# The feed-forward's first product with half of its chunk pairs as seven block products, and sums moved to GpSimd and ScalarE

## The chip, the cores and the metric

The kernel runs on one core of one Trainium2 chip. The metric is the device time of one execution in microseconds, lower is better; the times given are medians of several runs. The engines are TensorE (PE in the profile; its weight loads are listed as PEld), VectorE (DVE), ScalarE (ACT), GpSimd (POOL) and SyncE (SP), which issues most DMAs. Each engine works through its own queue in program order.

## The reference

A block of a transformer on 4096 rows of 256 numbers, in fp32. The input is normalised to `xn`; the result is

```
out = x + attn_ref(xn) + ffn_ref(xn)

attn_ref:  x = layernorm(xn + windowed_attention(xn)) * gamma + beta
           h = gelu(x @ W1 + b1)          # 256 -> 1024
           return x + h @ W2 + b2         # 1024 -> 256

ffn_ref:   scores = softmax(xn @ gate_w.T + gate_b); the two best of 8 experts per row
           y = sum over them of  share * ((silu((xn@gw.T + gb) * (xn@uw.T + ub))) @ dw.T + db)
```

The change lies in the part of `attn_ref` behind the attention (the feed-forward, `gelu(x @ W1 + b1) @ W2`) and in how the experts' results are added to the output.

## The kernel before, in words

All products are fp32; TensorE runs each matmul of the program as two instructions. The kernel has three stages: a first one that normalises the rows, makes the logits and sorts rows by expert; a long middle one that interleaves the experts' units with the attention (the loop over `ALWAYS` blocks, followed by five units that are skipped or run by a flag); and a last one, the feed-forward, which is the loop `for g in range(NG)` at line 1547 with eight groups of 512 rows. The order of the work on every engine is the order in which the program is written (`manual_schedule`, line 140): no planner moves anything.

In the last stage, a group g passes through these steps, and the loop is skewed so that three groups are at work at once:

- `second_loads` (line 1186), two iterations ahead: SP loads `x2`, the attention's output with the residual (two buffers), and `acc`, the rows of the kernel's input, in which the output is summed (four buffers).
- `second_norm` (line 1190): ScalarE applies the layer norm to `x2`, in four activations of 128x256.
- `turned2` (line 1209): TensorE transposes `x2` into two PSUM banks, and ScalarE writes them to `x2T` with gamma and beta.
- `hidden` (line 1222), the first product: eight chunks of 128 hidden units; each is two matmuls with 512 columns into a bank `ph` of its own, followed by a gelu on ScalarE from PSUM to `hT`.
- `second_base` (line 1202): VectorE adds `beta + b2` and `gamma * x2` to `acc`, in three instructions of 128x1024.
- `picked` (line 1266): GpSimd issues eight indirect gathers per group, which fetch each row's two expert results from `done` into tiles `got` of 128x256 (eight buffers, so a group's gathers wait until VectorE has used up the group before).
- `combined` (line 1281): VectorE multiplies each gathered tile by the row's share and adds it to `acc`, in eight instructions of 128x256.
- `sums_of_hidden` (line 1254) and `second` (line 1289): the second product, one group late, as seven products of blocks with a quarter of the size instead of eight (Winograd's form of Strassen's method). Its weight sums `V2` are made once on GpSimd (line 1248, at block `STEPS + 1`); VectorE makes four sums of 128x1024 of the hidden layer per group, and adds the products to `acc`.
- `store`: SP writes `acc` out.

PSUM has a pool of seven banks that the program takes in turn (`bank`, line 129), and one more for the attention. `hidden`, `turned2` and `second` together take 8 + 2 + 7 banks per group.

GpSimd can't begin the gathers of group 0 before the last flagged unit's results are stored; the zeroing of those units' buffers (line 1517) precedes them in its queue.

Of the kernel before, what the change touches and what calls it, by code (L numbers as in the profile page):

```python
# [32 lines left out]
F32 = mybir.dt.float32  # L33
# [3 lines left out]
ALU = mybir.AluOpType  # L37
# [66 lines left out]
def block_kernel(ctx: ExitStack, tc: tile.TileContext, a: dict, out: bass.AP):  # L104
# [1071 lines left out]
    def second_rows(g):  # L1176
        x2 = accp.tile([P, TG, D], F32, tag="x2", name=f"x2_{g}", bufs=2)
        nc.sync.dma_start(out=x2, in_=rows(x1d, g * TG, TG))
        return x2
# [22 lines left out]
    def second_base(g, acc, x2):  # L1202

        scaled = accp.tile([P, TG, D], F32, tag="scaled", name=f"scaled{g}", bufs=1)
        nc.vector.tensor_tensor(acc, acc, bcast(beta_b2, TG, 1), ALU.add)
        nc.vector.tensor_tensor(scaled, x2, bcast(gamma, TG, 1), ALU.mult)
        nc.vector.tensor_tensor(acc, acc, scaled, ALU.add)

    def turned2(g, x2):
        x2T = turns.tile([P, DC, G], F32, tag="x2T", name=f"x2T{g}")  # L1210
        for c in range(DC):
            pt = bank(f"pt2_{g}_{c}")
            for t in range(TG):
                nc.tensor.transpose(  # L1214
                    pt[:, t * P : (t + 1) * P], x2[:, t, c * P : (c + 1) * P], ident
                )
            nc.scalar.activation(
                x2T[:, c, :], pt, AF.Identity, bias=beta_c[:, c : c + 1], scale=gamma_c[:, c : c + 1]
            )
        return x2T  # L1220

    def hidden(g, x2T):
        hT = hf.tile([P, FC1, G], F32, tag="hf", name=f"hf{g}")
        for f in range(FC1):
            ph = bank(f"ph{g}_{f}")
            for c in range(DC):
                nc.tensor.matmul(  # L1227
                    ph,
                    W1[:, c, f * P : (f + 1) * P],
                    x2T[:, c, :],  # L1230
                    start=(c == 0),
                    stop=(c == DC - 1),
                )
            nc.scalar.activation(hT[:, f, :], ph, AF.Gelu, bias=b1[:, f : f + 1])  # L1234
        return hT

# [11 lines left out]
    def sums_of_weights():  # L1248
        b11, b12, b21, b22 = W2[:, F_LO, C1], W2[:, F_LO, C2], W2[:, F_HI, C1], W2[:, F_HI, C2]
        t1, t2, t3, t4 = (V2[:, k] for k in range(4))  # L1250
        for out_, left_, right_ in ((t1, b12, b11), (t2, b22, t1), (t3, b22, b12), (t4, b21, t2)):
            nc.gpsimd.tensor_tensor(out_, left_, right_, ALU.subtract)
# [12 lines left out]

    def picked(g):

        ys = []
        for i in range(g * TG, (g + 1) * TG):
            for k in range(2):  # L1270
                y = got.tile([P, D], F32, tag="got", name=f"got{i}_{k}")
                nc.gpsimd.indirect_dma_start(  # L1272
                    out=y,
                    out_offset=None,
                    in_=done,
                    in_offset=bass.IndirectOffsetOnAxis(ap=slot[:, k, i : i + 1], axis=0),
                )
                ys.append(y)
        return ys

    def combined(g, acc, ys):
        for n, y in enumerate(ys):
            t, k = n // 2, n % 2
            i = g * TG + t
            nc.vector.scalar_tensor_tensor(  # L1285
                acc[:, t, :], y, share[:, k, i : i + 1], acc[:, t, :], ALU.mult, ALU.add
            )

    def second(g, acc, hT, v):

        t1, t2 = slice(0, 2), slice(2, 4)
        u = hf.tile([P, 2, P], F32, tag="u", name=f"u{g}")

        def product(n, left, right):
            pb = bank(f"s{g}_{n}").rearrange("p (t n) -> p t n", n=P)[:, 0:2]
            for t in range(2):
                for f in range(FH):
                    nc.tensor.matmul(  # L1298
                        pb[:, t, :],
                        left[:, f, t * P : (t + 1) * P],  # L1300
                        right[:, f, :],
                        start=(f == 0),
                        stop=(f == FH - 1),
                    )
            return pb

        def add(t, cols, pb):
            nc.vector.tensor_tensor(acc[:, t, cols], pb, acc[:, t, cols], ALU.add)  # L1308

        p1 = product(1, hT[:, F_LO, 0:B], W2[:, F_LO, C1])  # L1310
        nc.scalar.copy(u, p1)  # L1311
        add(t1, C1, u)
        yield
        p2 = product(2, hT[:, F_HI, 0:B], W2[:, F_HI, C1])
        add(t1, C1, p2)
        yield
        p6 = product(6, v[:, 1], V2[:, 1])
        nc.vector.tensor_tensor(u, p6, u, ALU.add)
        add(t1, C2, u)
        yield  # L1320
        p5 = product(5, v[:, 0], V2[:, 0])
        add(t1, C2, p5)
        add(t2, C2, p5)
        yield
        p7 = product(7, v[:, 2], V2[:, 2])
        nc.vector.tensor_tensor(u, p7, u, ALU.add)
        add(t2, C1, u)
        add(t2, C2, u)
        yield
        p3 = product(3, v[:, 3], W2[:, F_HI, C2])  # L1330
        add(t1, C2, p3)
        yield
        p4 = product(4, hT[:, F_HI, B:], V2[:, 3])
        add(t2, C1, p4)
        yield
# [35 lines left out]
    for b in range(ALWAYS):  # L1371
# [63 lines left out]
        if b == STEPS:  # L1435
            att.close()
            wf = pool(ctx, "wf", right)
            accp = pool(ctx, "accp", right, bufs=4)
            V2 = wf.tile([P, 4, FC1 // 2, P], F32, tag="V2", name="V2")
            x2s = {n: second_rows(n) for n in range(2)}  # L1440
            W1, W2 = matrix(wf, "W1", F1, DC), matrix(wf, "W2", D, FC1)
            b1 = column("b1", FC1, wf)
            gamma, beta, b2 = (row(n, D, wf) for n in ("gamma", "beta", "b2"))
            gamma_c, beta_c = column("gamma_c", DC, wf), column("beta_c", DC, wf)
            beta_b2 = wf.tile([P, D], F32, tag="beta_b2", name="beta_b2")
            shift2 = wf.tile([P, NT], F32, tag="shift2", name="shift2")
            turns = pool(ctx, "turns", right, bufs=2)

            late = pool(late_done, "late", right)
            other.update({n: late for n in range(ALWAYS, BLOCKS, 3)})  # L1450
            load_unit(ALWAYS)
            for n in range(ALWAYS, BLOCKS):
                xs[n] = gather(n)
            x2s = {n: (second_inputs(n), x2) for n, x2 in x2s.items()}
        if b == STEPS + 1:
            sums_of_weights()
        if b == ALWAYS - 1:
            load_unit(ALWAYS + 1)
        if b + 1 < ALWAYS:
# [52 lines left out]


    x2Ts = {n: turned2(n, x2s[n][1]) for n in range(2)}

    for b in range(ALWAYS, BLOCKS):
        nc.gpsimd.memset(xs[b], 0.0)
# [18 lines left out]
    late_done.close()  # L1536
    experts_done.close()
    hf = pool(ctx, "hf", right, bufs=2)
    got = pool(ctx, "got", right, bufs=8)
    second_base(0, *x2s[0])  # L1540
    last = None

    def some(steps, n):
        for _ in range(n):
            next(steps, None)

    for g in range(NG):
        if g + 2 < NG:
            x2s[g + 2] = second_loads(g + 2)
        hT = hidden(g, x2Ts.pop(g))  # L1550
        if g + 1 < NG:
            second_base(g + 1, *x2s[g + 1])
        if g > 0:
            acc = x2s.pop(g - 1)[0]
            combined(g - 1, acc, ys)
        if 0 < g < NG - 1:
            x2Ts[g + 1] = turned2(g + 1, x2s[g + 1][1])
        if g + 2 < NG:
            second_norm(g + 2, x2s[g + 2][1])
        ys = picked(g)  # L1560
        outs = second(g - 1, acc, *last) if g > 0 else iter(())
        some(outs, 2)
        sums = sums_of_hidden(g, hT)
        last = hT, next(sums)
        some(outs, 2)
        some(sums, 1)
        some(outs, 3)
        if g > 0:
            store(g - 1, 0, TG, acc)
    acc = x2s.pop(NG - 1)[0]  # L1570
    combined(NG - 1, acc, ys)
    outs = second(NG - 1, acc, *last)
    some(outs, 6)
    store(NG - 1, 0, 2, acc)
    some(outs, 1)
    store(NG - 1, 2, 2, acc)
# [86 lines left out]
```

## Time and profile before

| | |
|---|---|
| median of 3 runs | 1070.18 us (1069.54 to 1071.64) |
| the profiled execution | 1067.22 us, span 1065.5 us |
| the last stage within the span | from 846.8 us to the end |
| ScalarE per gelu from PSUM, 128x512 | 0.687 us |
| VectorE per sum of 128x1024 | 1.22 us |
| VectorE per weighted add of 128x256 (line 1285) | 0.482 us |
| GpSimd per gather of the last stage | 1.008 us in the mean |

The profile is of one execution. A row of a timeline gives the start, the duration, the engine, the line in the kernel, the operation, and output and inputs by the program's names; in brackets follows how long the engine had been idle and what released it. In the chain in order of time the columns are start, duration, engine, tile, line and the number of instructions. A matmul's duration holds its pipeline too, so the distance from start to start tells its cost in a dense run.

### The profile page before, as it was taken

The page shows a single profiled execution, that of the slowest core. Times are in us where ns is not written, and L with a number is a line of the kernel's source. Part 1 is how long each engine was busy: PE and PEld are TensorE (multiplying, and loading weights), DVE is VectorE, ACT ScalarE, POOL GpSimd, SP SyncE. Part 2 cuts the span into 40 slices and gives each one's busy share as a digit, 9 for nine tenths or more (in the row PEclk, how much of TensorE's full clock was granted, in tenths as well). Part 3 has the DMA queues.
Part 4 walks back from the last instruction along what each step waited for, and adds up shares of the span by engine and source line. Part 5 has one row for each costly group of instructions (what it writes and reads, how often), then busy time and mean ns, then how long its engine had stood idle before and what let it go on. Part 6 is the DMA issues. An engine that isn't in the chain of part 4 may idle for free. (4 is left out here: it accounts for less than half of the span.)

```text
span 1065.5 us, 20424 instructions
## 1 busy us (share of the span) xinstructions
PE 1056.0 (99%) x7278; PEld 859.9 (81%) x7278; DVE 755.9 (71%) x1852; ACT 572.0 (54%) x1329; POOL 586.8 (55%) x706
## 2 busy tenths in 40 slices
PE   9999999999999999999999999999999999999998
PEld 6578887887888888888888888888888757777778
DVE  6667876877787687788888988888542455555546
ACT  4527566656656557756665666566454353333320
POOL 5418765675666666776777777777520053222220
PEclk9999999999999999999999999999999999999999
DMA  8226444435345344534543544445585343333111
GB/s 282 81 91 217 140 158 164 165 139 184 120 155 187 111 156 164 193 139 166 173 168 130 189 163 165 139 173 179 179 272 179 134 136 109 100 99 98 61 60 41
DMA packets 61047, 158.67 MB, mean 149 GB/s; under 512 B 6576, under 2 KB 46896, under 8 KB 56208
## 3 DMA queue, kind: packets, MB, share of 16 engines
q1 hardware_dynamic: 53632, 139.33, 37.7%
q0 software_dynamic: 6480, 17.70, 5.2%
q8 instruction: 59, 0.97, 0.4%
q10 hardware_dynamic: 832, 0.30, 0.1%
q14 instruction: 44, 0.36, 0.1%
HBM read 135.43 MB, written 21.89 MB: 148 GB/s over the span
## 5 line engine op out<-in xcount | busy, mean ns | idle before, releaser
L839 PE MATMUL gu<-xsT,wg 128*128 128x256 f32 (+1 forms) x1632 | 362.8, 369 | 0.0
L839 PEld LDWEIGHTS gu<-xsT,wg 128*128 128x128 f32 x1632 | 288.8, 190 | 46.0 <-DVE nm L1057 9.0
L1272 POOL DMA_INDIRECT got<-done,slot x64 | 64.5, 1008 | 175.8 <-DVE acc L1285 106.9
L847 ACT ACTIVATE gs<-gu,wg 128x256 f32<-128x256 f32 (+1 forms) x204 | 92.0, 452 | 112.8 <-PE gu L839 108.4
L1084 POOL TENSOR_TENSOR pr<-pr 128x256 f32<-128x256 f32 x128 | 113.5, 887 | 64.1 <-ACT pr L1072 64.1
L848 DVE SCALAR_TENSOR_TENSOR hT<-gu,wg,gs 128x256 f32<-128x256 f32 (+1 forms) x204 | 91.9, 462 | 73.8 <-ACT gs L847 73.8
L1085 POOL TENSOR_TENSOR pr<-pr,ident 128x256 f32<-128x256 f32 x128 | 132.8, 1038 | 10.0
L1072 ACT ACTIVATE pr<-pr,nm 128x256 f32<-128x256 f32 x256 | 126.8, 497 | 1.0 <-ACT xsT L831 0.6
L1227 PE MATMUL ph<-x2T,W 128*128 128x512 f32 x256 | 111.0, 592 | 0.0
L1234 ACT ACTIVATE hf<-ph,b 128x512 f32<-128x512 f32 x64 | 43.8, 687 | 122.0 <-PE ph L1227 55.3
L880 ACT ACTIVATE hT<-hT 128x512 f32<-128x512 f32 (+2 forms) x179 | 84.9, 485 | 32.6 <-DVE hT L848 22.4
L1057 DVE CUSTOM_DVE_ANT_0 pr<-ps,mask 128x256 f32<-128x256 f32 x256 | 90.7, 420 | 16.1 <-PE ps L1043 16.1
L814 POOL DMA_INDIRECT xs<-xnd,token x71 | 68.8, 969 | 50.7 <-DVE paired_tiles L781 33.1
L1227 PEld LDWEIGHTS ph<-x2T,W 128*128 128x128 f32 x256 | 48.2, 190 | 57.9 <-issue 54.5
L1102 DVE TENSOR_TENSOR pr<-pr,rec 128x1024 f32<-128x1024 f32 x32 | 39.2, 1225 | 42.5 <-POOL pr L1084 42.5
L1115 POOL TENSOR_TENSOR xd<-xd,same 128x256 f32<-128x256 f32 x32 | 19.7, 615 | 84.2 <-DVE same L1113 84.1
L1308 DVE TENSOR_TENSOR acc<-u,acc 128x256 f32<-128x256 f32 x32 | 12.9, 423 | 68.4 <-ACT u L1311 67.9
L929 POOL TENSOR_TENSOR ts<-wd 128x384 f32<-128x384 f32 x54 | 54.0, 1000 | 2.1
L1072 ACT ACT_TABLE_LOAD x31 | 39.8, 1283 | 19.3 <-DVE nm L1057 19.3
L973 ACT COPY y<-sh 128x512 f32<-128x512 f32 x27 | 15.8, 586 | 62.3 <-PE sh L952 62.3
L1072 ACT ACTIVATION_READ_ACCUMULATOR pr<-pr,nm 128x1 f32 x256 | 48.3, 189 | 0.0
L952 PE MATMUL pe<-wd,hT 128*128 128x128 f32 x324 | 44.9, 275 | 0.0
(252 smaller groups left out, 2114.7 us busy)
## 6 DMA issues: line engine op xcount, KB each, us to landing
wg<-in_gate_up SPq DMA_DIRECT2D x37, 1670.5 KB, 7.1
wd<-in_down SPq DMA_DIRECT2D x37, 896.0 KB, 4.7
done<-y SPq DMA_DIRECT2D x30, 256.0 KB, 2.1
x<-in_x SPq DMA_DIRECT2D x8, 512.0 KB, 5.6
xnd<-xn SPq DMA_DIRECT2D x8, 512.0 KB, 4.9
res<-xnd SPq DMA_DIRECT2D x16, 256.0 KB, 2.9
x1d<-res SPq DMA_DIRECT2D x16, 256.0 KB, 2.2
x<-x1d SPq DMA_DIRECT2D x8, 512.0 KB, 4.7
```

The lines of the kernel that those rows point to most:

```text
L814: nc.gpsimd.indirect_dma_start(out=x[:, t, :], out_offset=None, in_=xnd, in_offset=bass.IndirectOffsetOnAxis(ap=token[:, i : i + 1], axis=0),)
L839: nc.tensor.matmul(pb[:, k, :], w[:, lo : lo + P], xT[:, c, :], start=(c == 0), stop=(c == DC - 1),)
L847: nc.scalar.activation(gs, pb[:, 0, :], AF.Identity, bias=w[:, gb : gb + 1])
L848: nc.vector.scalar_tensor_tensor(hT[:, f, :], pb[:, 1, :], w[:, ub : ub + 1], gs, ALU.add, ALU.mult)
L880: nc.scalar.activation(hT[on, lo:hi, :], hT[on, lo:hi, :], AF.Silu)
L929: nc.gpsimd.tensor_tensor(out_, left_, right_, ALU.subtract)
L1057: nc.vector.tensor_tensor_reduce(out=pr[:, hh, j, :], in0=ps[hh][:, j, :], in1=mask[:, kinds[j], :], scale=-1.0, scalar=-LOWEST, op0=ALU.a ...
L1072: nc.scalar.activation(pr[:, hh, j, :], pr[:, hh, j, :], AF.Exp, bias=nm[:, j, hh : hh + 1], scale=-1.0, accum_out=sums[:, j, hh : hh + 1],)
L1084: nc.gpsimd.tensor_tensor(first, first, second, ALU.add)
L1085: nc.gpsimd.tensor_tensor(second, second, bcast(ident, 2, 1), ALU.mult)
L1227: nc.tensor.matmul(ph, W1[:, c, f * P : (f + 1) * P], x2T[:, c, :], start=(c == 0), stop=(c == DC - 1),)
L1272: nc.gpsimd.indirect_dma_start(out=y, out_offset=None, in_=done, in_offset=bass.IndirectOffsetOnAxis(ap=slot[:, k, i : i + 1], axis=0),)
```

## The change

In `hidden`, the eight chunks are taken in four pairs. Pairs 0 and 2 are computed as before. For pairs 1 and 3 the product of the 256x256 weight block with the 256x512 input is made by seven products of 128x128 blocks with 256 columns each, in place of eight; they go to seven halves of four banks. This needs four sums of the weights (`V1`, made once, on GpSimd) and four sums of the input per group (`sums_of_inputs`, on GpSimd, behind `turned2`). The seven products are put together by one copy on ScalarE and five sums on VectorE, which write into `hT`; the gelus of such a pair then run in place on `hT`, behind the next pair's matmuls in the program or, for pair 3, behind the first part of `second`.

`second_base` moves from VectorE (three instructions of 128x1024) to GpSimd (twelve of 128x256). The scaling of the gathered expert results moves to ScalarE (`weighted`: eight activations of 128x256 per group, dealt out between the pairs of `hidden`), and VectorE adds them in two instructions of 128x1024. The gathers get one tile per group with two buffers. In `second`, VectorE's adds of the products p5 and p7 to two places each become one instruction each. The order in the loop changes: `picked` comes directly behind `hidden`, `second_base` of the next group behind it, then `turned2` and `sums_of_inputs` of the next group.

```diff
     def second_base(g, acc, x2):
         scaled = accp.tile([P, TG, D], F32, tag="scaled", name=f"scaled{g}", bufs=1)
-        nc.vector.tensor_tensor(acc, acc, bcast(beta_b2, TG, 1), ALU.add)
-        nc.vector.tensor_tensor(scaled, x2, bcast(gamma, TG, 1), ALU.mult)
-        nc.vector.tensor_tensor(acc, acc, scaled, ALU.add)
+        for t in range(TG):
+            a_, s_ = acc[:, t, :], scaled[:, t, :]
+            nc.gpsimd.tensor_tensor(s_, x2[:, t, :], gamma, ALU.mult)
+            nc.gpsimd.tensor_tensor(a_, a_, beta_b2, ALU.add)
+            nc.gpsimd.tensor_tensor(a_, a_, s_, ALU.add)
...
+    def sums_of_first_weights():
+        m = blocks_of_first()
+        a11, a12, a21, a22 = m[:, 0, 0], m[:, 0, 1], m[:, 1, 0], m[:, 1, 1]
+        s1, s2, s3, s4 = (V1[:, k] for k in range(4))
+        nc.gpsimd.tensor_tensor(s1, a21, a22, ALU.add)
+        for out_, left_, right_ in ((s2, s1, a11), (s3, a11, a21), (s4, a12, s2)):
+            nc.gpsimd.tensor_tensor(out_, left_, right_, ALU.subtract)
+
+    def sums_of_inputs(g, x2T):
+        ts = turns.tile([P, 4, B], F32, tag="x2s", name=f"x2s{g}")
+        b11, b12, b21, b22 = x2T[:, 0, 0:B], x2T[:, 0, B:], x2T[:, 1, 0:B], x2T[:, 1, B:]
+        t1, t2, t3, t4 = (ts[:, k] for k in range(4))
+        for out_, left_, right_ in ((t1, b12, b11), (t2, b22, t1), (t3, b22, b12), (t4, b21, t2)):
+            nc.gpsimd.tensor_tensor(out_, left_, right_, ALU.subtract)
+        return x2T, ts
...
+        def gelu(m):
+            for f in range(2 * m, 2 * m + 2):
+                nc.scalar.activation(hT[:, f, :], hT[:, f, :], AF.Gelu, bias=b1[:, f : f + 1])
+
+        for m in range(FC1 // 2):
+            if m % 2 == 0:
+                pbs = [bank(f"ph{g}_{m}_{k}") for k in range(2)]
+                for k, pb in enumerate(pbs):
+                    for c in range(DC):
+                        nc.tensor.matmul(
+                            pb, w[:, k, c, m, :], x2T[:, c, :], start=(c == 0), stop=(c == DC - 1)
+                        )
+                if m > 0:
+                    gelu(m - 1)
+                for k, pb in enumerate(pbs):
+                    f = 2 * m + k
+                    nc.scalar.activation(hT[:, f, :], pb, AF.Gelu, bias=b1[:, f : f + 1])
+                for _ in range(2 if m == 0 else 1):
+                    next(others, None)
+                continue
+            banks = [halves(bank(f"ph{g}_{m}_{k}")) for k in range(4)]
+            p1, p6, p7, p5, p2, p4, p3 = (banks[k // 2][:, k % 2, :] for k in range(7))
+            for to, left_, right_ in (
+                (p1, w[:, 0, 0, m, :], x2T[:, 0, 0:B]),
+                (p6, V1[:, 1, m, :], ts[:, 1]),
+                (p7, V1[:, 2, m, :], ts[:, 2]),
+                (p5, V1[:, 0, m, :], ts[:, 0]),
+                (p2, w[:, 0, 1, m, :], x2T[:, 1, 0:B]),
+                (p4, w[:, 1, 1, m, :], ts[:, 3]),
+                (p3, V1[:, 3, m, :], x2T[:, 1, B:]),
+            ):
+                nc.tensor.matmul(to, left_, right_, start=True, stop=True)
+
+            q = hf.tile([P, 3, B], F32, tag="q", name=f"q{g}_{m}", bufs=3)
+            both = hT[:, 2 * m : 2 * m + 2, :]
+            nc.scalar.copy(q[:, 0], p1)
+            nc.vector.tensor_tensor(q[:, 1], p6, q[:, 0], ALU.add)
+            nc.vector.tensor_tensor(q[:, 2], p7, q[:, 1], ALU.add)
+            nc.vector.tensor_tensor(both[:, :, B:], q[:, 1:3], bcast(p5, 2, 1), ALU.add)
+            nc.vector.tensor_tensor(both[:, :, 0:B], banks[2], q[:, 0::2], ALU.add)
+            nc.vector.tensor_tensor(both[:, 0, B:], p3, both[:, 0, B:], ALU.add)
+            next(others, None)
+        return hT, lambda: gelu(FC1 // 2 - 1)
...
+    def weighted(g, ys):
+        for t in range(TG):
+            for k in range(2):
+                i = g * TG + t
+                nc.scalar.activation(
+                    ys[:, k, t, :], ys[:, k, t, :], AF.Copy, scale=share[:, k, i : i + 1]
+                )
+            yield
+
+    def combined(acc, ys):
+        for k in range(2):
+            nc.vector.tensor_tensor(acc, acc, ys[:, k], ALU.add)
...
     for g in range(NG):
         if g + 2 < NG:
             x2s[g + 2] = second_loads(g + 2)
-        hT = hidden(g, x2Ts.pop(g))
+        hT, ended = hidden(g, *x2Ts.pop(g), weighted(g - 1, ys) if g > 0 else iter(()))
+        ys_last = ys if g > 0 else None
+        ys = picked(g)
         if g + 1 < NG:
             second_base(g + 1, *x2s[g + 1])
+        if 0 < g < NG - 1:
+            x2Ts[g + 1] = sums_of_inputs(g + 1, turned2(g + 1, x2s[g + 1][1]))
+        acc = x2s.pop(g - 1)[0] if g > 0 else None
         if g > 0:
-            acc = x2s.pop(g - 1)[0]
-            combined(g - 1, acc, ys)
-        if 0 < g < NG - 1:
-            x2Ts[g + 1] = turned2(g + 1, x2s[g + 1][1])
+            combined(acc, ys_last)
+        outs = second(g - 1, acc, *last) if g > 0 else iter(())
+        some(outs, 1)
+        ended()
         if g + 2 < NG:
             second_norm(g + 2, x2s[g + 2][1])
-        ys = picked(g)
-        outs = second(g - 1, acc, *last) if g > 0 else iter(())
-        some(outs, 2)
+        some(outs, 1)
         sums = sums_of_hidden(g, hT)
```

Behind the loop, the last group's eight scalings stand in front of its `second`, and its `combined` behind the first two products. `sums_of_first_weights` is called at block `STEPS + 1`, behind `sums_of_weights`; the first two groups' `sums_of_inputs` stand behind their `turned2` at line 1514, in front of the zeroing at line 1517.

More of the change, by code (lines that the diff above doesn't have):

```diff
@@ L1220, in turned2, with blocks_of_first @@
         return x2T
-    def hidden(g, x2T):
-        hT = hf.tile([P, FC1, G], F32, tag="hf", name=f"hf{g}")
[L1224 to L1235, printed above, removed]
+    def blocks_of_first():
+        return W1.rearrange("p c (m e q) -> p e c m q", e=2, q=P)
@@ new lines, in hidden @@
+    def hidden(g, x2T, ts, others):
+        hT = hf.tile([P, FC1, G], F32, tag="hf", name=f"hf{g}")
+        w = blocks_of_first()
+        def gelu(m):
[39 more added lines that the diff above has]
+        return hT, lambda: gelu(FC1 // 2 - 1)
@@ L1266, in picked @@
     def picked(g):
-        ys = []
-        for i in range(g * TG, (g + 1) * TG):
+        ys = got.tile([P, 2, TG, D], F32, tag="got", name=f"got{g}")
+        for t in range(TG):
+            i = g * TG + t
             for k in range(2):
-                y = got.tile([P, D], F32, tag="got", name=f"got{i}_{k}")
                 nc.gpsimd.indirect_dma_start(
-                    out=y,
+                    out=ys[:, k, t, :],
                     out_offset=None,
@@ L1277, in picked @@
                 )
-                ys.append(y)
         return ys
[L1281 to L1287, printed above, removed]
+    def weighted(g, ys):
+        for t in range(TG):
+            for k in range(2):
+                i = g * TG + t
+                nc.scalar.activation(
[5 more added lines that the diff above has]
+            nc.vector.tensor_tensor(acc, acc, ys[:, k], ALU.add)
     def second(g, acc, hT, v):
@@ L1321, in second @@
         p5 = product(5, v[:, 0], V2[:, 0])
-        add(t1, C2, p5)
-        add(t2, C2, p5)
+        right = acc.rearrange("p (k t) d -> p k t d", k=2)[:, :, :, C2]
+        nc.vector.tensor_tensor(right, right, bcast(p5, 2, 1), ALU.add)
         yield
@@ L1326, in second @@
         nc.vector.tensor_tensor(u, p7, u, ALU.add)
-        add(t2, C1, u)
-        add(t2, C2, u)
+        low = acc[:, t2, :].rearrange("p t (h n) -> p t h n", h=2)
+        nc.vector.tensor_tensor(low, low, bcast(u, 2, 2), ALU.add)
         yield
@@ L1439, in block_kernel @@
             V2 = wf.tile([P, 4, FC1 // 2, P], F32, tag="V2", name="V2")
+            V1 = wf.tile([P, 4, FC1 // 2, P], F32, tag="V1", name="V1")
             x2s = {n: second_rows(n) for n in range(2)}
@@ L1456, in block_kernel @@
             sums_of_weights()
+            sums_of_first_weights()
         if b == ALWAYS - 1:
@@ L1514, in block_kernel @@
     x2Ts = {n: turned2(n, x2s[n][1]) for n in range(2)}
+    x2Ts = {n: sums_of_inputs(n, x2T) for n, x2T in x2Ts.items()}
     for b in range(ALWAYS, BLOCKS):
@@ L1538, in block_kernel @@
     hf = pool(ctx, "hf", right, bufs=2)
-    got = pool(ctx, "got", right, bufs=8)
+    got = pool(ctx, "got", right, bufs=2)
     second_base(0, *x2s[0])
@@ L1570, in block_kernel @@
     acc = x2s.pop(NG - 1)[0]
-    combined(NG - 1, acc, ys)
+    list(weighted(NG - 1, ys))
     outs = second(NG - 1, acc, *last)
-    some(outs, 6)
+    some(outs, 2)
+    combined(acc, ys)
+    some(outs, 4)
     store(NG - 1, 0, 2, acc)
```

## The prediction

> **What bounds the kernel now.** I read the page's busy times, then the chain in order of time, then the engines' timelines in the last stage, and last the groups by shape.
>
> ```profile
> PE 1056.0 (99%) x7278; PEld 859.9 (81%) x7278; DVE 755.9 (71%) x1852; ACT 572.0 (54%) x1329; POOL 586.8 (55%) x706
> ```
>
> TensorE is busy throughout. The chain says where that decides:
>
> ```profile
> 846.76 27.47 PE ph L1227 x64
> 874.22 0.87 PE pt L1214 x8
> 875.10 12.51 PE s L1298 x112
> 887.60 13.73 PE ph L1227 x32
> ...
> 1023.18 13.73 PE ph L1227 x32
> 1036.92 25.03 PE s L1298 x224
> 1061.94 0.02 issue
> 1061.97 0.42 DVE acc L1308
> ```
>
> From 846.8 to 1062 us one TensorE piece follows another: the first product (ph), turns (pt), the second product (s), 13.73 + 0.87 + 12.51 = 27.11 us for a group of 512 rows, without a gap. Everything else there is covered today, so whatever shortens TensorE shortens the kernel, unless another engine's cover is used up. So I look at GpSimd and VectorE:
>
> ```profile
> 850.15 1.50 POOL L1272 DMA_INDIRECT got<-done,slot  x1 [56.10 <-DVE scaled L1206]
> 851.95 1.94 POOL L1272 DMA_INDIRECT got<-done,slot  x1 [0.30 <-issue]
> 854.20 0.95 POOL L1272 DMA_INDIRECT got<-done,slot  x1 [0.30 <-issue]
> ...
> 860.46 0.95 POOL L1272 DMA_INDIRECT got<-done,slot  x1 [0.30 <-issue]
> 870.20 1.07 POOL L1272 DMA_INDIRECT got<-done,slot  x1 [8.80 <-DVE acc L1285]
> ```
>
> GpSimd does nothing here but issue eight gathers a group, one each 1.25 us (0.95 and a 0.30 gap), 10 us of 27. It can't begin before the experts' last results are stored, at 850.2.
>
> ```profile
> 256.51 0.72 POOL L1084 TENSOR_TENSOR pr<-pr 128x256 f32<-128x256 f32 x1
> 257.26 1.23 DVE L1102 TENSOR_TENSOR pr<-pr,rec 128x1024 f32<-128x1024 f32 x1 [0.22 <-POOL pr L1084]
> 257.31 1.77 POOL L1085 TENSOR_TENSOR pr<-pr,ident 128x256 f32<-128x256 f32 x1
> ```
>
> A GpSimd sum of 128x256 takes 0.72 us alone, and 1.77 us where it starts just behind a 1024-wide VectorE sum of two SBUF tensors: it stands still for 1.0 us, most of that instruction.
>
> **The change, part by part.** *TensorE.* Two of a group's four chunk pairs change from 8 instructions of 512 columns to 14 of 256. The 512s follow each other at 13.73/32 = 0.429 us. For 256s I take the expert units' dense run at line 839: 48 from 810.72 to 821.17, 0.218 us. So 3.43 becomes 3.05: 0.38 saved, 16 times, 6.1 us in all; a group is then 26.35 us. With nothing in the way: 1067.2 - 6.1 = 1061.1 in the profiled execution's terms (span 1065.5 and 1.7 around it), and 1064.1 against the median of 1070.2, which lies 3.0 above.
>
> *ScalarE.* For eight gelus from PSUM (0.687 each) come four from PSUM, four from SBUF (about 0.63, by the silu of that shape, line 880), two copies (0.364, line 1311) and eight scalings of 128x256 (0.52, by line 1194: four in 2.07). With line 1217's two (1.44), line 1194's four and one u copy, 14 us of 26. No table load lies between gelu and copy in the trace. The order matters more: block copy p1 stands behind two gelus and four scalings, so in a group that starts at 0 it comes at 6.4 (its product ended at 3.9), VectorE's five sums end at 9.4, the pair's gelus at 10.8, the next plain pair's at 12.0. TensorE needs that last bank at 13.8 for the second product. So 1.6 us of slack; in group 1, where norms and gelus crowd, it is gone, and I take 0.2 us there.
>
> *VectorE.* Off it go second_base (three times 1.22) and eight 0.48 sums; onto it come ten block sums (0.42 for 256, 0.68 for 512 from PSUM, by lines 1308 and 1124), about 5.3 us, and two 1.22 sums. About 17 of 26 us: covered.
>
> *GpSimd* is the part that I cost at more than nothing. A group adds twelve base sums and four input sums of 128x256. Rows for such a sum: 0.615 (line 1115, an operand repeated), 0.73 with 0.75 start to start (lines 1084 and 1085 alone); 128 and 384 wide start 0.415 and 1.07 apart, between them 0.74. I take 0.74, ends 0.68 and 0.75. So a group needs 10.0 + 16 x 0.74 = 21.8 us alone. To it come the standstills: VectorE's sums of two SBUF tensors are six of 1024 (four for the hidden layer, two of combined), 1.0 us each, two of 256 at 0.3 and one of 512 at 0.5: 7.1 us if all meet a GpSimd sum. Block sums have one operand in PSUM, and GpSimd's 384-wide sums stay at 1.00 beside VectorE's PSUM work (lines 929 and 1057), so they cost nothing. Bounds for the group: 21.8 and 28.9.
>
> Would gathers be stopped too? The Trainium skill (SBUF — State Buffer, "Who interferes with whom") infers that tensor_tensor doesn't hold back descriptor generation. The rows above differ: the two gathers under lines 1205 to 1207 took 1.50 and 1.94 instead of 0.95, some 0.5 us per VectorE sum; yet one at 879.33 beside line 1258 took 0.94. By the rule gathers stay 1.25 apart; by the first rows group 1's set costs 1.5 us more. I follow the rule, since most gathers will lie beside block sums.
>
> *When it bites: the input sums of group 2.* They stand last in GpSimd's queue. From 850.2: gathers of group 0, 10.0, to 860.2; base of group 1, 8.9, with the four hidden sums of group 0 falling into it, 4.0, to 873.1; gathers of group 1 to 883.1; base of group 2, 8.9 + 2.8 (two hidden sums and the smaller ones), to 894.8; the second input sum, 1.5, at 896.3. TensorE wants it for its second block product: 846.8 + 12.97 (group 0) + 26.35 + 0.2 + 3.87 = 890.2. **A stall of 6.1 us.** Even without standstills GpSimd would be there only at 889.5. Behind that product stand all of TensorE's later work and, through its banks, ScalarE and VectorE.
>
> *After that.* Having once waited for GpSimd, TensorE runs a fixed distance behind it: the next gathers lie under the block sums, and combined, hidden sums and adds all fall into the next base sums. By the sum, 28.9; a walk through one group's order gives 28.7 with 0.74 and 27.5 to 27.9 with quicker sums. I take 28.2, so 28.2 - 26.35 = 1.85 us of waiting in each of groups 3 to 7, 9.3 us.
>
> *Hidden.* The V1 sums (four 512-wide, 1.3 each, line 1252) and the first two input sums (5.9) run in GpSimd's idle time from 795 to 850; base of group 0 follows and ends near 825; the zeroing passed by them is needed at 822.7 by the first store and is done by 815. Without that cover they would push the first gathers. SP's x2 loads now wait for GpSimd's base sums, which in the walk are done some 12 us before the norm on ScalarE. The merged adds save VectorE about a microsecond, off the path. The tail keeps its order: last product, add, store.
>
> The sum: -6.1 + 0.2 + 6.1 + 9.3 = +9.5, or **1079.7 us** against the median, and 1076.7 for a profiled execution.
>
> A second rule speaks against the change: by the skill (TensorE: Matmul & The Clock Gate, Part 1) an idle window of about 3.4 us halves the clock until TensorE was busy as long. The granted clock is 1.00 in every stretch of this stage, which has no such pause; my 6.1 us one would be the first. At half clock for 3.4 us it costs an estimated 1.7. While GpSimd sets the pace TensorE has that to spare, so 9.5 stands; where TensorE sets it, add 1.7.
>
> **The rivals.** *GpSimd keeps up.* If VectorE mostly finds GpSimd between sums, or sums take 0.6, group 2's inputs come in time, only ScalarE's 0.2 remains, and the time is 1064. For it: 21.8 us of need against 26.35. Against: the 1.77 row, and that 889.5 against 890.2 leaves no room. *One stall and no more:* with half the standstills (groups of 25.4 us) the stall is 2.7 to 5, -6.1 + 0.2 + 4 + up to 1.7, around 1070. This decides at a GpSimd group under 26.35, that is standstills under 4.5 us. *ScalarE sets the pace:* if scalings or SBUF gelus cost about 0.3 more each, the 1.6 us of slack is passed in each group; at 2 us more, 8 x 2 - 6 = +10 without GpSimd, and up to 1090 with it. The copies between gelus in the trace speak against it. *That the block products don't save:* weights load in 0.19 us, under 0.218; at 0.245 each nothing would be left. Dense 256s at 0.218 exclude it.
>
> **How the numbers follow.** GpSimd sets the pace 0.53 (its own range 1075 to 1086: sums of 0.68, a 5 us stall and 27.5, or 7.5 us and 28.9); GpSimd keeps up 0.18; one stall 0.20, of which 0.05 faster, 0.08 within, 0.07 slower; ScalarE 0.09. Within 0.2% (2.1 us, about what a measurement of this kernel can tell from none) 0.08; faster 0.18 + 0.05 = 0.23; slower 0.69. The range from 1065 to 1087 leaves out the lower part of the second case and the upper ends of the first and last, under 2 in 10.
>
> **What would show it.** In the chain of the changed kernel: GpSimd's input sums ahead of the ph pieces from group 2 on; TensorE waiting for ts near 890, for 4 to 8 us, then 1 to 2.5 us a group; GpSimd busy nearly all of 850 to 1010; base sums with a mean near 1.0 and single ones near 1.77; block products 0.218 apart. A gapless TensorE chain with 26.35 us groups would prove me wrong, as would TensorE waiting for gelus or u copies instead.

## The result

| | median | runs | ratio to before |
|---|---|---|---|
| before | 1070.12 us (1069.54 to 1071.64) | 4 | |
| after | 1078.57 us (1078.12 to 1078.83) | 4 | 1.0077, 95% interval 1.0063 to 1.0091 |

The change makes the kernel slower by 8.4 us; 1079.7 was predicted. The profiled execution of after took 1078.55 us, at its median (span 1076.8); that of before lay 3 us under its own median, so the two spans differ by 11.3 us. 1.5 of these lie ahead of the last stage, where both kernels run the same TensorE work: in the chain the first product starts at 848.30 now, at 846.76 before.

**The page of after**, busy times and the row of the granted TensorE clock:

```profile
PE 1056.8 (98%) x7374; PEld 880.3 (82%) x7374; DVE 773.1 (72%) x1844; ACT 601.0 (56%) x1409; POOL 719.3 (67%) x838
...
PEclk9999999999999999999999999999999998999999
```

GpSimd went from 55% to 67%, and TensorE from 99% to 98% with less to do. For the first time there is a slice at 8 in the clock's row.

**The chain of after in order of time** was a gapless row of TensorE pieces before. From 874 to 1038.6 us it is now GpSimd's (start, duration, engine, tile, line; other links are left out):

```profile
POOL 13%; PE 6%; issue 2%; DVE 0%; POOLq 0%
...
927.79 0.99 POOL got L1332
...
955.89 0.99 POOL got L1332
...
984.01 0.99 POOL got L1332
...
1012.16 0.99 POOL got L1332
...
1038.64 3.11 PE ph L1284 x12
1041.75 3.43 PE ph L1262 x8
1045.18 3.02 PE ph L1284 x14
1048.21 25.02 PE s L1362 x224
```

The first gathers of successive groups start 28.10, 28.12 and 28.15 us apart. TensorE takes over only for the last first product and the tail. The last two ph rows give the saving: seven block products in 3.02 us, a plain pair in 3.43.

**GpSimd's timeline of after** shows where 28.1 us come from:

```profile
862.84 0.73 POOL L1209 TENSOR_TENSOR acc<-acc,scaled 128x256 f32<-128x256 f32 x1
863.53 0.73 POOL L1207 TENSOR_TENSOR scaled<-x,gamma 128x256 f32<-128x256 f32 x1
864.22 1.76 POOL L1208 TENSOR_TENSOR acc<-acc,beta_b 128x256 f32<-128x256 f32 x1
...
874.12 0.99 POOL L1332 DMA_INDIRECT got<-done,slot  x1
875.42 0.95 POOL L1332 DMA_INDIRECT got<-done,slot  x1 [0.30 <-issue]
```

Some sums take 0.73 us, and some, beside a 1024-wide VectorE sum of two SBUF tensors, 1.59 to 1.78: the means of the three base sums are 1.21, 1.26 and 1.12 us. VectorE is slowed in return: its four sums of the hidden layer, 1.22 us each before, take 1.26 to 1.68 in the mean (1.22 again in the run below that leaves the base sums on VectorE). The gathers keep 1.25 us from start to start.

**TensorE's timeline of after** has three things in it: short pauses with no wait shown, one wait followed by slow products, and one wait a group from group 5 on:

```profile
882.74 0.27 PE L1362 MATMUL s<-V,hv 128*128 128x128 f32 x1 [0.17 <-issue]
883.47 0.27 PE L1362 MATMUL s<-V,hv 128*128 128x128 f32 x1 [0.46 <-issue]
884.85 0.39 PE L1362 MATMUL s<-V,hv 128*128 128x128 f32 x2 [1.12 <-issue]
885.59 2.06 PE L1362 MATMUL s<-V,hv 128*128 128x128 f32 x17 [0.35 <-issue]
...
898.57 2.93 PE L1284 MATMUL ph<-x2s,V 128*128 128x256 f32 x6 [3.48 <-POOL x2s L1243]
901.29 1.06 PE L1284 MATMUL ph<-x2T,W 128*128 128x256 f32 x2
...
908.16 1.46 PE L1284 MATMUL ph<-x2s,V 128*128 128x256 f32 x6
...
982.55 1.82 PE L1284 MATMUL ph<-x2s,V 128*128 128x256 f32 x6 [1.31 <-POOL x2s L1243]
...
1010.70 1.82 PE L1284 MATMUL ph<-x2s,V 128*128 128x256 f32 x6 [1.33 <-POOL x2s L1243]
...
1038.64 1.82 PE L1284 MATMUL ph<-x2s,V 128*128 128x256 f32 x6 [1.13 <-POOL x2s L1243]
```

The wait of group 2 is 3.48 us, for the input sums, as foretold in kind. Behind it the same six instructions take 2.93 us instead of 1.46. The waits of groups 5 to 7 cost more than their brackets: the sums then come some 0.7 us apart, and the six instructions need 1.82.

**Stretches of after around that wait** (per stretch: length, busy time of PE, PEld, DVE, ACT and POOL with instructions, granted clock, DMA share, GB/s):

```profile
894.00:898.00 4.00, 1.09 (x4) 0.38 (x2) 0.94 (x3) 2.28 (x5) 3.84 (x6) 0.99 0.48 140
898.00:904.00 6.00, 5.43 (x13) 4.32 (x14) 2.23 (x4) 1.18 (x3) 4.94 (x7) 0.50 0.66 213
904.00:908.00 4.00, 4.00 (x11) 1.78 (x10) 0.42 (x1) 2.10 (x4) 3.09 (x4) 0.91 0.36 102
908.00:914.00 6.00, 6.00 (x44) 5.62 (x43) 4.13 (x7) 3.51 (x8) 5.59 (x7) 1.00 0.21 66
```

The clock is at half from 897.90 to 904.72, for 6.8 us. From 898.57 to the next first block product at 907.72 TensorE needed 9.15 us for work that takes 12 x 0.216 + 3.43 = 6.02 at full clock: 3.1 us lost.

### The profile page after: what moved, and what is told of

Same layout as the page of the kernel before. It is cut to its first block, busy times and chain, and to the rows that moved or that the text cites. A ratio compares the mean times of both kernels' runs of the same rounds, so it can differ in the third digit from the quotient of the medians.

```text
span 1076.8 us, 20832 instructions
## 1 busy us (share of the span) xinstructions
PE 1056.8 (98%) x7374; PEld 880.3 (82%) x7374; DVE 773.1 (72%) x1844; ACT 601.0 (56%) x1409; POOL 719.3 (67%) x838
## 5 line engine op out<-in xcount | busy, mean ns | idle before, releaser
L1332 POOL DMA_INDIRECT got<-done,slot x64 | 60.9, 952 | 48.1 <-issue 47.1
L1262 PE MATMUL ph<-x2T,W 128*128 128x512 f32 x128 | 58.0, 596 | 0.0
L1269 ACT ACTIVATE hf<-ph,b 128x512 f32<-128x512 f32 x32 | 21.3, 680 | 61.4 <-PE ph L1262 60.1
L1289 DVE TENSOR_TENSOR q<-ph,q 128x256 f32<-128x256 f32 x16 | 6.8, 424 | 61.9 <-ACT q L1288 36.2
L1362 PE MATMUL s<-V,hv 128*128 128x128 f32 x384 | 44.8, 275 | 2.1 <-issue 2.1
L1362 PEld LDWEIGHTS s<-V,hv 128*128 128x128 f32 x384 | 43.8, 192 | 2.4 <-issue 2.0
```

The lines of the kernel that those rows point to most:

```text
L1262: nc.tensor.matmul(pb, w[:, k, c, m, :], x2T[:, c, :], start=(c == 0), stop=(c == DC - 1))
L1332: nc.gpsimd.indirect_dma_start(out=ys[:, k, t, :], out_offset=None, in_=done, in_offset=bass.IndirectOffsetOnAxis(ap=slot[:, k, i : i + 1] ...
L1362: nc.tensor.matmul(pb[:, t, :], left[:, f, t * P : (t + 1) * P], right[:, f, :], start=(f == 0), stop=(f == FH - 1),)
```

## The experiments

The theory: GpSimd's need for a group is over TensorE's, and TensorE waits for the input sums, which stand last in GpSimd's queue. Rivals: something else slows TensorE, and the waits for GpSimd would otherwise be filled by it; or another part of the change costs the time.

**The base sums back on VectorE.** All else of the change stays.

```diff
-        for t in range(TG):
-            ...   (three sums of 128x256 on nc.gpsimd)
+        nc.vector.tensor_tensor(acc, acc, bcast(beta_b2, TG, 1), ALU.add)
+        nc.vector.tensor_tensor(scaled, x2, bcast(gamma, TG, 1), ALU.mult)
+        nc.vector.tensor_tensor(acc, acc, scaled, ALU.add)
```

> The changed kernel with the base sums back on VectorE, in three instructions of 128x1024 at the same place. GpSimd then has 10.0 us of gathers and 3.0 us of input sums a group, and VectorE about 21 of 26 us. GpSimd theory: no wait for input sums, 1064 to 1068. ScalarE theory: 1077 to 1080. If VectorE becomes the bound by the 3.6 us that come back to it, TensorE waits for banks that block sums hold, some 0.5 to 1 us a group: 1070 to 1075.

1062.67 us against 1068.58, ratio 0.9944 (0.9928 to 0.9961). The waits of TensorE in the last stage are this one line (total us, times, longest):

```profile
PE pt L1214 <- ACT hf L1267: 0.7, 1, 0.7
```

Groups are 26.3 us apart. VectorE, busy for 21.7 of 27 us, is not in the way. Run once more:

> The version with the base sums on VectorE once more beside the others, to tell small differences: 1061.5 to 1064 beside a kernel before of 1067 to 1070.

1062.22 us, 0.9956 (0.9943 to 0.9970). So the base sums on GpSimd turn a gain of 5 to 6 us into a loss of 8.4.

**The base sums alone moved to GpSimd**, in the kernel before:

> The kernel before with one part of the change alone: the base sums on GpSimd in twelve instructions; products, gathers, adds and their order as before. GpSimd theory: 10.0 us of gathers, 8.9 of sums and up to 7 of standstills are under the 27.1 us of a group, and nothing that TensorE needs soon stands behind them; 1068 to 1072. If moving the base sums is costly as such: 1076 to 1080.

1067.59 us against 1067.35, ratio 1.0003 (0.9994 to 1.0012). There nothing on TensorE waits for GpSimd, and the same move costs nothing. It is the input sums behind the base sums that give GpSimd's queue a reader on the path.

**One more base sum a block** (four a group):

```diff
-            nc.gpsimd.tensor_tensor(s_, x2[:, t, :], gamma, ALU.mult)
+            for _ in range(2):
+                nc.gpsimd.tensor_tensor(s_, x2[:, t, :], gamma, ALU.mult)
```

> The changed kernel with the product of x2 and gamma made twice on GpSimd: 16 base sums a group for 12, the same output. GpSimd theory with 0.74 us a sum: 2 x 4 x 0.74 = 5.9 us later at group 2 and 5 x 3.0 us after it, 14.7, together 20.7: 1097 to 1101, with a GpSimd group of 31.1 us. ScalarE theory, or any in which GpSimd is hidden: 1078 to 1080.

1097.93 us, ratio 1.0271 (1.0253 to 1.0288). TensorE's timeline in this run:

```profile
901.56 2.93 PE L1285 MATMUL ph<-x2s,V 128*128 128x256 f32 x6 [10.36 <-POOL x2s L1244]
...
932.57 1.95 PE L1285 MATMUL ph<-x2s,V 128*128 128x256 f32 x6 [1.87 <-POOL x2s L1244]
```

Every group from 2 on now waits, and gathers start about 30.9 us apart. Four more sums a group lengthen it by 2.8 us: what GpSimd gets, the kernel pays.

**More VectorE work of two kinds**, behind p5's add, to tell the standstill apart from VectorE's own load: two 1024-wide sums of an SBUF tile with itself (1.60 us each as measured, 3.2 a group), or six 256-wide sums with p5 in PSUM (0.417 each, 2.5 a group). The first edit, then the second (the tile `spare` is made and zeroed ahead of the loop):

```diff
+        for _ in range(2):
+            nc.vector.tensor_tensor(spare, spare, spare, ALU.add)
```

```diff
+        for n in range(6):
+            w_ = spare[:, n % TG, :].rearrange("p (t n) -> p t n", t=2)
+            nc.vector.tensor_tensor(w_, p5, w_, ALU.add)
```

> The changed kernel with two more VectorE sums of 128x1024 a group behind the add of p5, both operands in SBUF (a tile of zeros added to itself), the same output. VectorE has the time: some 21 of 28 us a group. [...]each stops a GpSimd sum for 1.0 us, so group 2's inputs come 2 us later and each of the five groups behind it takes 2 us more: 10 to 12 us, 1088 to 1091. If the long GpSimd sums of the profile have another cause (a slow form, or the two sums' dependence), VectorE's idle time takes the new work: 1078 to 1080.

> The control to the two sums of SBUF tensors: in their place six VectorE sums of 128x256 of about the same time together (2.1 us a group), each with one operand in PSUM (the product p5) and one in SBUF. [...]they don't stop GpSimd, 1078 to 1081. If added VectorE time in itself is what delays GpSimd or TensorE: 1088 to 1091, as with the two sums.

The first: 1088.16 us, 1.0191 (1.0174 to 1.0209). The second: 1077.03 us, 1.0094 (1.0077 to 1.0111), which overlaps the change's own interval. The waits of the first, then of the second:

```profile
PE ph L1284 <- POOL x2s L1243: 19.0, 7, 8.7
```

```profile
PE ph L1284 <- POOL x2s L1243: 10.7, 4, 7.0
```

Gathers start 29.8 us apart in the first, 28.0 in the second. VectorE's added time is not far apart, 3.2 and 2.5 us; it costs GpSimd 0.9 us per 1024-wide sum where the operands are in SBUF, and nothing where one is in PSUM. So the standstill goes with VectorE's sums of SBUF tensors, as the prediction took from one row, and not with VectorE's load (though the two kinds differ in width as well).

**The input sums ahead of the base sums**, so that TensorE finds them early although GpSimd has the same work:

```diff
         ys = picked(g)
-        if g + 1 < NG:
-            second_base(g + 1, *x2s[g + 1])
         if 0 < g < NG - 1:
             x2Ts[g + 1] = sums_of_inputs(g + 1, turned2(g + 1, x2s[g + 1][1]))
+        if g + 1 < NG:
+            second_base(g + 1, *x2s[g + 1])
```

> The changed kernel with two lines of the loop exchanged: the next group's input sums stand in front of its base sums in GpSimd's queue, so that TensorE's block products wait for 8 gathers and 4 sums where they waited for 12 sums more. Nothing is left out. GpSimd theory: group 2's inputs are ready near 887 where TensorE asks near 893, and GpSimd's lag of about 1.8 us a group never uses up the 12 us gained; no wait for the input sums, no half clock, a time of 1064 to 1068. If it is GpSimd's load as such that sets the pace, whatever stands last (a group of 28.1 us against 26.3), the waits come back by the last groups: 1070 to 1074. ScalarE theory (its scalings and the gelus in place delay the banks): 1077 to 1080, as before the exchange.

1069.14 us against 1068.58, ratio 1.0003 (0.9994 to 1.0011): over what was expected. The waits for the input sums are gone and the clock is 1.00 throughout, but TensorE's waits are now

```profile
PE s L1362 <- issue: 4.0, 8, 0.9
PE pt L1216 <- ACT hf L1269: 0.5, 1, 0.5
```

and the groups from group 1 on are 3.4, 1.1, 1.3, 0.7, 0.0 and 0.7 us over 26.3. 1.1 of the first lie in its turns, as with the base sums on VectorE (27.39 us there); for the other 6.1 us the trace shows no wait. The pauses are all in the second product, like those at 882.7 in after.

**Block products that read the turned input itself.** Left out: the input sums as operands, so the hidden layer is another one; GpSimd still makes the sums, and nobody waits for them.

```diff
-                (p6, V1[:, 1, m, :], ts[:, 1]),
+                (p6, V1[:, 1, m, :], x2T[:, 0, B:]),
```

(p7, p5 and p4 likewise.)

> The changed kernel with the four block products that read input sums reading blocks of the input itself instead; every sum is still made on GpSimd, with the same instructions on every engine, but TensorE doesn't need them. Left out: the use of the input sums, so the hidden layer is another one. GpSimd theory: TensorE's groups are 26.3 us throughout, 1064 to 1068, and GpSimd's queue still takes about 28 us a group. ScalarE theory: 1077 to 1080.

1068.56 us, ratio 0.9999 (0.9990 to 1.0008): missed in the same way. No waits for GpSimd; 3.0 us of pauses without a releaser in six places, and behind the first two of them the clock at half for 3.4 us (884.46 to 887.87). So the theory covers the waits, but in these two runs a second cost shows once the waits are gone.

**Where does the second cost come from?** The record gives the chip of each run but after: both of these were on chip 10, those below on 12 and 7. In both runs these pauses lie around the end of a group's eight gathers (in the run with the input sums first, from 1.0 us before the eighth ends to 1.6 behind), while TensorE is in the second product. The next idea was that gathers under the second product starve TensorE. So, with the base sums on VectorE, the gathers were moved there on purpose:

```diff
-        ys = picked(g)
         if g + 1 < NG:
             second_base(g + 1, *x2s[g + 1])
         if 0 < g < NG - 1:
             x2Ts[g + 1] = sums_of_inputs(g + 1, turned2(g + 1, x2s[g + 1][1]))
+        ys = picked(g)
```

> The version with the base sums on VectorE, with one more move: GpSimd issues a group's gathers behind the next group's input sums in place of ahead of them, so that they run some 17 to 27 us behind a group's start, under the dense second product, and no longer under the first. The same instructions, the same output. Theory that TensorE's instructions come late while gathers run under the second product (the gaps of 0.4 to 1 us without a wait that the traces of the two versions without input waits show there, some 0.7 us a group): gaps come back in groups 1 to 6, 1066 to 1069. If those gaps belong to the base sums on GpSimd beside TensorE's reads, none come: 1062 to 1064. If instead the scalings wait for their gathers, ScalarE stands in front of the block copies and the time is 1064 to 1072, but with waits that the trace puts down to gathers.

1061.95 us against 1067.48, ratio 0.9954 (0.9939 to 0.9970), and no pause: the idea fell as it stood, as far as a run on another chip can tell. But the gathers were not the same ones. GpSimd's timeline there:

```profile
879.63 1.77 POOL L1330 DMA_INDIRECT got<-done,slot  x1
881.71 0.95 POOL L1330 DMA_INDIRECT got<-done,slot  x1 [0.30 <-issue]
```

12 of 56 gathers from group 1 on take over 1.3 us, as those two rows show one that does and one that doesn't; in after none of 64 does.

The same with plain loads in place of the gathers (left out: the choice of rows, so other rows of the experts' results are added):

> As the late gathers, but each gather is a plain load of the same size (128 rows of 1 KB) on ScalarE's queue. Left out: the choice of rows, so other experts' results are added. If the bytes moved under the second product hold up TensorE's instructions, the gaps stay, 1065 to 1070; if it is the gathers' own descriptors[...], they go, 1062 to 1064.

1061.38 us, 0.9947 (0.9931 to 0.9962), no pauses either, as with gathers; this pair tells nothing apart.

The order that does have the pauses, input sums first, was then run with plain loads instead of gathers. Left out again: the choice of rows.

```diff
-                nc.gpsimd.indirect_dma_start(out=ys[:, k, t, :], ...)
+                nc.scalar.dma_start(out=ys[:, k, t, :], in_=done[i * P : (i + 1) * P, :])
```

> As the run with the input sums first, but the gathers of the other experts' rows are plain loads of 128 rows each on ScalarE's queue at the same place. Left out: the choice of rows, so other rows of the experts' results are added. If the gathers issued by GpSimd at full pace under the second product are the ingredient of TensorE's gaps there: the gaps (4.0 us in 8) go, and the time is 1062 to 1065 us. If the base sums on GpSimd beside the other engines' reads are enough: the gaps stay, 1067 to 1070 us.

1061.08 us against 1067.54, ratio 0.9939 (0.9922 to 0.9955). First TensorE's second product of group 0, then two stretches:

```profile
877.53 5.52 PE L1357 MATMUL s<-V,hv 128*128 128x128 f32 x48
...
901.00:928.00 27.00, 27.00 (x173) 22.42 (x172) 19.01 (x28) 12.93 (x26) 16.91 (x16) 1.00 0.33 102
928.00:955.00 27.00, 27.00 (x173) 22.42 (x172) 19.02 (x26) 13.17 (x27) 17.39 (x17) 1.00 0.35 107
```

and the same two of the run with gathers:

```profile
901.00:928.00 27.00, 26.08 (x164) 21.52 (x163) 18.09 (x25) 12.17 (x25) 24.32 (x25) 1.00 0.35 108
928.00:955.00 27.00, 26.25 (x163) 21.39 (x162) 17.81 (x25) 11.97 (x25) 24.01 (x26) 1.00 0.35 105
```

The 48 matmuls with hv run in one piece, TensorE is never idle, and no pause is left, though the base sums are on GpSimd, the order is the same and the DMAs move about as many bytes a second. This points at the gathers, but it doesn't show them to be an ingredient. The run with the pauses was on another chip (10) than this one (7), and without gathers GpSimd's sums also begin some 3 us earlier within a group. A run on a third chip (6) speaks against it: the one with six PSUM sums is the changed kernel, gathers and all, up to the first sum that was added. TensorE there, and then one of GpSimd's gathers:

```profile
877.09 5.52 PE L1362 MATMUL s<-V,hv 128*128 128x128 f32 x48
...
897.01 2.93 PE L1284 MATMUL ph<-x2s,V 128*128 128x256 f32 x6 [6.95 <-POOL x2s L1243]
```

```profile
877.54 1.85 POOL L1332 DMA_INDIRECT got<-done,slot  x1 [0.30 <-issue]
```

The 48 matmuls that take 8.2 us in after, from 879.40 on, take 5.5 here without a pause, and two of the gathers beside them are held (1.85 and 1.88 us; in after none is). The run with two more SBUF sums, on the same chip, has no such pauses either. Nor are the pauses common to chip 10: the runs there with the base sums on VectorE and with four more base sums have none.

The trace shows one thing more: around a pause TensorE's word that a product is done comes late. In after, VectorE adds the product p2, the second half of the first row here, 5.3 us after its end, though VectorE was free from 882.28 on. In the run with the input sums first, the product p1 that began at 931.4 ended at 933.3, and ScalarE, idle since 932.6, copies it at 937.27:

```profile
875.72 3.84 PE L1362 MATMUL s<-W,hf 128*128 128x128 f32 x32
884.90 0.42 DVE L1372 TENSOR_TENSOR acc<-s,acc 128x256 f32<-128x256 f32 x1 [2.62 <-remote]
```

```profile
937.27 0.37 ACT L1375 COPY u<-s 128x256 f32<-128x256 f32 x1 [4.67 <-remote]
```

Semaphores are the counters by which the engines tell each other what is done. The traces record TensorE's updates only just ahead of these two starts, at 884.87 and 937.25. The traces of after and of the four runs on chip 10 also lack 30 to 90 of some 600 semaphore updates in the last stage; those of all other runs lack none. So the pauses go with late and missing semaphore updates. Whether they belong to the kernel, to one chip or to the recording of the trace stays open: the order with the input sums first was run with its gathers on one chip only.

**One more pair as block products** (pairs 1, 2 and 3), with the base sums on VectorE; each block pair's gelus follow the next pair's sums:

```diff
-            if m % 2 == 0:
+            if m == 0:
```

> The version with the base sums on VectorE, with pairs 1, 2 and 3 of each group as block products in place of 1 and 3; the same output. By the block products' measured spacing 0.41 us less in each group, 3.3 us in all: 1059.5 against the 1062.7 of two pairs. Against it VectorE's 2.7 us more a group, about 24 of 25.9 us: where block sums then come late for the banks, 1062 to 1068.

1060.47 us against 1067.48, ratio 0.9931 (0.9918 to 0.9945). It is the lowest ratio of the runs that compute the whole layer, and faster than both kernels; against the version with two pairs (0.9944, 0.9956) the intervals overlap, so the third pair's own gain isn't shown. TensorE has 1.7 us of waits for VectorE's block sums, in group 1:

```profile
PE ph L1279 <- DVE hf L1286: 1.3, 1, 1.3
PE ph L1279 <- DVE q L1284: 0.4, 1, 0.4
```

Behind these two waits the clock is at half for 3.4 us (from 872.00 on; the rows are in the last section), an estimated 1.7 us more. So in group 1 the third pair gives back most of the 3.3 us that were forecast for it.

## Why the prediction was right

The sum was -6.1 + 0.2 + 6.1 + 9.3 = +9.5. The time came out within 1.1 us, and by the mechanism that was named. The terms:

*The block products, -6.1.* 3.43 - 3.02 = 0.41 a pair, 6.6 us. Right; and with neither waits nor pauses the change does gain this much: the run with the input sums first and plain loads has a ratio of 0.9939, 6.5 us.

*ScalarE, +0.2.* One wait for a bank in group 1, 0.58 us. Right in place, somewhat small. There is no other: the rival that ScalarE sets the pace is out.

*GpSimd's queue up to group 2.* The walk, with what was measured: gathers of group 0 end at 860.2 (861.3), base of group 1 at 873.1 (874.1), gathers at 883.1 (883.9), base at 894.8 (897.0), the second input sum at 896.3 (898.5). The later start accounts for the first microsecond; the base of group 2 took 13.1 us and not 11.7, since two more of its sums met a standstill.

*The stall, +6.1.* Here the sum was mis-sized: 3.48 us. The step that failed is "846.8 + 12.97 (group 0) + 26.35 + 0.2 + 3.87 = 890.2". TensorE asked at 895.1: 1.5 us from the later start, 0.4 from the bank, and 2.8 because its second product of group 0 took 15.3 us and not 12.5, through the pauses, which no step of the prediction had. GpSimd came 2.2 us later than forecast, so 6.1 + 2.2 - 4.9 = 3.4. The pauses cost nothing here, since TensorE would have waited for GpSimd instead. In the run with six PSUM sums, which has no pauses, TensorE asks at 890.05 and gets the sums at 897.01, where the forecast had 890.2 and 896.3: a wait of 6.95 us.

*The clock.* The rule of the Trainium skill (TensorE: Matmul & The Clock Gate, Part 1) was put at 1.7 us. This case agrees that a pause halves the clock and differs in the size: 3.1 us, since the clock stayed at half for 6.8 us and not 3.4. That it would be to spare held: GpSimd's period stayed at 28 us, and TensorE, 3 us behind, met no wait of note in groups 3 and 4.

*1.85 us in each of groups 3 to 7, +9.3.* The step per group is confirmed nearly to the digit: GpSimd needs 28.1 us (28.2 said), and with TensorE's 26.3 the groups that waited were longer by 1.83, 1.84 and 1.65. It came in groups 5 to 7 only, with half a microsecond in group 4. So the waits came to some 9 us and not 15.4, and pauses and half clock took the rest of the time. The end didn't change, because it was counted along GpSimd's queue: 896.3 + 5 x 28.2 = 1037.3 said for the last input sums, 1038.6 found, with a start 1.5 later.

*Gathers.* Taking them as not held back, by the rule (SBUF — State Buffer, "Who interferes with whom"), fits after: 0.952 us in the mean, none of the 64 over 1.3, even beside combined's two sums at 879.3 to 881.8. As a rule it does not hold here: beside the same two sums, gathers took 1.85 and 1.88 us in the run with six PSUM sums, and with the gathers moved behind the input sums, 12 of 56 took up to 1.87 us.

*The rivals.* "GpSimd keeps up" (1064) is what one gets with the base sums on VectorE. What the prediction lacked is that removing the waits alone would not get there: with TensorE no longer waiting, it would have said 1064 to 1068, and 1069.1 was measured, level with before on that chip.

## What to carry to other kernels

When work moves to an engine with idle time, add up that engine's period including standstills and compare it with the bound's; then look at what stands last in its queue, for that decides whether the surplus is paid. Moving the sums cost nothing in the kernel before and 13 to 14 us where TensorE read a tile made behind them. A forecast made along the queue that becomes the bound survives errors about the other engines; the split into their waits does not, and taking one wait away may uncover the next cost. A control for such a cost has to run where the cost was seen: on another chip it may be missing for another reason.

## What the runs showed of the hardware

- **Pauses far below 3.4 us halve the clock, and it is a matter of where they lie.** Within the last stage of each trace the clock stays at half for 3.41 us or a multiple of it, and its changes are multiples of 3.41 us apart (in the run with four more base sums it falls at 934.12, 964.84 and 995.56, nine times 3.41 apart each time). Stretches of that length, in the run with four more base sums (a pause of 1.87 us) and in the one with three pairs (pauses of 0.43 and 1.26 us):

```profile
930.71:934.12 3.41, 1.55 (x6) 1.09 (x7) 0.41 (x1) 2.69 (x8) 3.19 (x6) 1.00 0.85 238
934.12:937.53 3.41, 3.41 (x9) 2.46 (x8) 2.23 (x5) 0.36 (x1) 2.79 (x3) 0.50 0.68 211
```

```profile
868.59:872.00 3.41, 1.72 (x7) 0.90 (x6) 2.65 (x6) 0.00 (x0) 2.80 (x3) 1.00 0.35 106
872.00:875.41 3.41, 3.41 (x10) 2.69 (x9) 3.17 (x9) 2.87 (x6) 1.51 (x2) 0.50 0.43 115
```

  TensorE was busy for 1.55 and 1.72 us of the stretch ahead of the fall; in the run whose block products read the turned input itself it was 1.55, with pauses of 1.04 and 0.81. Where it was busy for 2.1 us or more (pauses of 1.1 to 1.4 us) the clock never fell. The border isn't sharp: a stretch with 1.60 us busy in the run with two more SBUF sums (a pause of 1.82) and one with 1.45 in the run with four more base sums were followed by full clock. The idle window of about 3.4 us of the Trainium skill (TensorE: Matmul & The Clock Gate, Part 1) fits the length of these stretches, but TensorE need not be idle throughout.
- **TensorE can pause, for up to 1.1 us at a time, with nothing to wait for that the trace shows.** In the run with the input sums first this went with some 6 us. All such pauses lie in after, in that run and in the one whose block products read the turned input itself, the latter two on one chip, and in traces that lack semaphore updates; the cause is open.
- **A gather can be held by VectorE as a sum is**: 1.77 us in place of 0.95, but only some of them; what decides which isn't settled by these runs.
